# Ten GpSimd no-operations in place of a memset between two row gathers in a graph layer on one Trainium2 core

## The chip, the cores and the metric

The kernel runs on one core of one Trainium2 chip. The metric is the device time of one execution in microseconds (us). Several executions are timed and their median is given; a separate execution is recorded by the hardware profiler, with the start and end of every instruction on every engine. TensorE (PE) multiplies matrices, VectorE (DVE) and ScalarE (ACT) do elementwise work, GpSimd (POOL) issues the indirect transfers, and SyncE (SP) issues the other transfers.

## The reference

The reference is one graph layer with a residual and a layer norm over 12,500 nodes of 128 features and 412,500 edges (200,000 random pairs in both directions and one loop for each node), sorted by the destination `dst`.

```python
theta = x[dst] - x[src]
w = sigmoid(relu(theta @ W1 + b1) @ W2 + b2)
agg = segment_sum(w * theta, dst, num_segments=n_nodes)
indeg = segment_sum(ones((dst.shape[0], 1)), dst, num_segments=n_nodes)
out = layernorm(x + agg + indeg * (x @ W4 + b4))
```

The random access is `x[src]`: for each edge a row of 128 features, and its product with `W1`, are needed beside the edge's other data.

## The kernel before

**Table.** The kernel first writes a table `z` to HBM with a row of 256 numbers for each node: `x @ W1` and `x`, side by side (1,024 bytes). It is made in chunks, by transposes and products on PE and copies on ACT.

**Parts.** The edges are worked in 260 parts, numbered `s`, from 0 to 259. The first 26 (`PLAIN`) hold 1,024 edges each in plain order. The other 234 hold 1,656 edges each: those whose source lies in a hot group of nodes that is kept in SBUF (`tabs`) are reached with one-hot products on PE, and the rest with gathers. Two parts make a block of destination nodes, which is normalised and written out at the block's end.

**Gathers.** The function `gather(s)` issues the row gathers of part `s`: eight indirect transfers on POOL for each part, but two for the last one. One gather brings 128 rows, one for each partition, into slot `k` of a buffer. The parts below `NH` = 8 gather 128 numbers a row straight from `x` while the table is still being written: 64 gathers, called x gathers here. All later parts gather 256 numbers a row from `z`: 2,010 gathers, called z gathers here, of which 144 belong to parts 8 to 25 and 1,866 to the parts from 26 on. The last 1,866 stand in the profile with the index tile `src_i`, the 144 with `src`.

**The rest.** Between each gather and the next, in all parts, `gather(s)` puts one more instruction on POOL, `rest` in the code. For an x gather it is one `engine_nop`, for a z gather a memset of the tile `rest_t`, 128 partitions by 320 float32 numbers, which nothing reads. A dependency without a semaphore (`NoSync`) fixes the order of gather, rest, gather on POOL.

**What sets the order around it.** POOL runs its instructions in the order in which they stand. In the main loop, `part(s)` with `s` from 26 on, `gather(s + LEAD)` is issued with `LEAD` = 3, so rows are fetched three parts ahead. Two things hold a gather back: its buffer, one of six (`zbuf`, a ring), must have been read by the part that used it before; and the first gather of a part waits for a recent PE instruction (`paced[s + LEAD] = newest[0]`), so that POOL cannot run far ahead. The orders of PE, DVE and ACT are written out by hand; the part's first DVE instruction on the gathered rows is at L896 (`nc.vector.tensor_sub(half, ...)`), and the last PE instructions on them are the sums at L1083. Beside the parts, DVE and ACT sort the edges of the next 128 parts into the hot and the gathered ones (`place`), a few instructions at a time.

Of the kernel before, what the change touches and what calls it, by code (L numbers as in the profile page):

```python
# [9 lines left out]
F32 = mybir.dt.float32  # L10
# [10 lines left out]
P = 128  # L21
# [19 lines left out]
NH = 8  # L41
# [39 lines left out]
def gnn_resnorm(  # L81
# [37 lines left out]
    nc = tc.nc  # L119
# [21 lines left out]
    const = ctx.enter_context(tc.tile_pool(name="const", bufs=1))  # L141
# [14 lines left out]
    def set_of(s):  # L156

        s0 = 0 if s < PLAIN else PLAIN + (s - PLAIN) // S2 * S2
        return placed[s0], s - s0
# [42 lines left out]
    def early(n, dtype=F32):  # L202

        a = used_of[0]
        used_of[0] = a + -(-n // (2 if dtype == BF16 else 1))
        assert used_of[0] <= HR * HT * D
        t = tabs_flat[:, a:used_of[0]]
        return t if dtype == F32 else t.bitcast(dtype)
# [47 lines left out]
    rest = early(D)  # L256
# [82 lines left out]
    def slots(s):  # L339
        return [h * J + j for h in range(2) for j in range(pairs(s))]  # L340
# [11 lines left out]
    def rows_of(s):  # L352
        return own_of(s)[:, :, :D] if s < NH else ring(s)[:, :, :2 * D]
# [8 lines left out]
        nc.vector.memset(zbuf[i][:, :, D + AW - 1:D + AW], 1.0)  # L362

    gathers = []
    rest_t = const.tile([P, 320], F32, name="rest_t")
    table_steps = []
    paced = {}

    def gather(s):

        (src_i, _, _), i = set_of(s)
        for k in slots(s):
            if gathers:
                rest = nc.gpsimd.memset(rest_t, 0.0) if s >= NH else nc.gpsimd.engine_nop()  # L374
                tc.add_manual_dep(
                    rest.ins, gathers[-1].ins.name,
                    mybir.DependencyInfo(mybir.DependencyClass.NoSync, mybir.DependencyReason.DATA),
                    reason="between two gathers")
                gathers.append(rest)
            ins = nc.gpsimd.indirect_dma_start(  # L380
                out=rows_of(s)[:, k, :], out_offset=None, in_=z if s >= NH else x,
                in_offset=IndirectOffsetOnAxis(ap=src_i[:, k, i:i + 1], axis=0))
            waits = [(gathers[-1], mybir.DependencyClass.NoSync)] if gathers else []
            at = (s * K + k) * 4 * len(chunks) // (NH * K) - 6
            if s < NH and 0 <= at < len(table_steps):
                waits.append((table_steps[at], mybir.DependencyClass.Sync))
            if k == 0 and s in paced:
                waits.append((paced[s], mybir.DependencyClass.Sync))
            for other, kind in waits:
                tc.add_manual_dep(  # L390
                    ins.ins, other.ins.name,
                    mybir.DependencyInfo(kind, mybir.DependencyReason.DATA), reason="gathers' pace")
            gathers.append(ins)
# [283 lines left out]
    with tc.manual_schedule(engines={SP}), tc.tile_pool(name="work", bufs=2) as wp, tc.tile_pool(  # L677
        name="ps_y", bufs=2, space=bass.MemoryType.PSUM
    ) as ps_y, tc.tile_pool(
        name="ps_l", bufs=1, space=bass.MemoryType.PSUM  # L680
# [518 lines left out]
        def gather_first():  # L1199

            while gathered[0] < AHEAD and (gathered[0] + 1) * len(chunks) <= (len(done) + 1) * NH:
                gather(gathered[0])
                gathered[0] += 1
# [63 lines left out]
        def early_part(s):  # L1267
# [21 lines left out]
            if h == 1:  # L1289
                load_dst((s + 3) // SUB)  # L1290
            gather(s + AHEAD)
            one_hot_w(s)
            logits(s)
# [49 lines left out]
        def part(s):  # L1343
# [26 lines left out]
            if PLAIN + AHEAD <= s + LEAD < NS:  # L1370
                if s >= PLAIN + 4:
                    paced[s + LEAD] = newest[0]
                gather(s + LEAD)
# [233 lines left out]
```

## Time and profile before

| what | value |
|---|---|
| median of 3 runs | 3409.33 us (3401.54 to 3410.72) |
| profiled execution, device time | 3395.38 us |
| its span, first to last instruction | 3393.6 us |
| mean granted TensorE clock | 0.885 |
| start of the first gather of part 26 | 386.90 us |
| start of the last gather | 3344.44 us |

A row of the timeline gives the start and the duration in us, the engine, the line of the kernel, the operation, the tile that is written and those that are read, the shape, and in brackets how long the engine was idle before it and what ended that. A row of the groups gives the number of instructions behind the x, then the busy time in us, the mean duration in ns, and behind the second bar the idle time of the engine before them with what ended it. POOLq is the sequencer of POOL: what stands there is not counted as busy time of the engine. "issue" marks idle time for which the profile shows no wait.

### The profile page before, as it was taken

The page shows a single profiled execution, that of the slowest core. Times are in us where ns is not written, and L with a number is a line of the kernel's source. Part 1 is how long each engine was busy: PE and PEld are TensorE (multiplying, and loading weights), DVE is VectorE, ACT ScalarE, POOL GpSimd, SP SyncE. Part 2 cuts the span into 40 slices and gives each one's busy share as a digit, 9 for nine tenths or more (in the row PEclk, how much of TensorE's full clock was granted, in tenths as well). Part 3 has the DMA queues.
Part 4 walks back from the last instruction along what each step waited for, and adds up shares of the span by engine and source line. Part 5 has one row for each costly group of instructions (what it writes and reads, how often), then busy time and mean ns, then how long its engine had stood idle before and what let it go on. Part 6 is the DMA issues. An engine that isn't in the chain of part 4 may idle for free.

```text
span 3393.6 us, 62355 instructions
## 1 busy us (share of the span) xinstructions
PE 2713.4 (80%) x18615; PEld 2351.2 (69%) x18615; DVE 2641.6 (78%) x6197; ACT 2363.5 (70%) x5856; POOL 2821.6 (83%) x4093
## 2 busy tenths in 40 slices
PE   6776778787788787888788878888878888888887
PEld 5676767676677676777677766676667777677776
DVE  6797458898888689888888858888887866666666
ACT  4554567776677677777777767777767777777774
POOL 5678778888888888888888888888888888888883
PEclk9876678898899888999898889899988999998998
DMA  7564434444444444444444444444444444444441
GB/s 255 184 169 121 119 93 121 118 111 117 121 113 120 128 113 116 121 117 121 122 118 120 116 118 123 117 117 124 116 115 123 115 122 117 119 122 118 126 110 55
DMA packets 265060, 416.67 MB, mean 123 GB/s; under 512 B 66608, under 2 KB 178217, under 8 KB 264205
## 3 DMA queue, kind: packets, MB, share of 16 engines
q0 software_dynamic: 98528, 267.78, 28.5%
q1 hardware_dynamic: 164219, 138.42, 15.6%
q10 hardware_dynamic: 1970, 6.40, 0.5%
q8 instruction: 154, 2.52, 0.3%
q14 instruction: 189, 1.55, 0.2%
HBM read 384.89 MB, written 27.49 MB: 122 GB/s over the span
## 4 chain that ended last, share of the span: by engine, by line
DVE 30%; ACT 25%; PE 16%; issue 11%; POOL 8%; DMA 5%; another core or an unknown queue 4%; DVEq 0%; SPq 0%; POOLq 0%; ACTq 0%
POOL zbuf L380 6%; ACT wxh L1063 5%; PE pd L980 4%; DVE hh L1054 4%; DVE zbuf L896 4%; DVE zbuf L898 4%; ACT zbuf L919 4%; DVE lg L899 4%; ACT of L966 4%; PE pa L1083 4%; POOL rest_t L374 2%; DMA zbuf<-z,src_i 2%; ACT of L968 2%; DVE ed L549 2%
## 5 line engine op out<-in xcount | busy, mean ns | idle before, releaser
L380 POOL DMA_INDIRECT zbuf<-z,src_i x1866 | 1816.1, 973 | 421.0 <-issue 261.6
L980 PE MATMUL pd<-of,tabs 128*128 128x128 f32 (+4 forms) x4816 | 685.9, 298 | 181.6 <-ACT of L968 95.8
L374 POOL MEMSET rest_t<- 128x320 f32 x2010 | 800.4, 398 | 1.0
L980 PEld LDWEIGHTS pd<-of,tabs 128*128 128x128 f32 x4816 | 628.9, 209 | 224.7 <-ACT of L968 113.5
L1083 PE MATMUL pa<-zbuf,ow 128*112 128x260 f32 (+1 forms) x2282 | 588.1, 406 | 47.6 <-ACT zbuf L919 21.6
L1083 PEld LDWEIGHTS pa<-zbuf,ow 128*112 128x112 f32 x2282 | 407.4, 200 | 157.7 <-ACT zbuf L919 30.1
L1025 PE MATMUL pxa<-wni,xT 128*128 128x128 f32 x1872 | 303.8, 311 | 258.0 <-DVE hh L1054 241.5
L1025 PEld LDWEIGHTS pxa<-wni,xT 128*128 128x128 f32 x1872 | 266.1, 218 | 281.8 <-DVE hh L1054 261.0
L966 ACT ACTIVATE of<-hot_src,nodes 128x512 f32<-128x512 f16 (+3 forms) x602 | 394.1, 709 | 7.1 <-issue 4.3
L919 ACT ACTIVATE zbuf<-zbuf 128x128 f32<-128x128 f32 x1144 | 362.8, 389 | 0.4
L1040 PE MATMUL y<-y,oh 64*128 64x128 f32 x1872 | 341.1, 323 | 14.2 <-issue 14.0
L1029 PE MATMUL pxa<-y,oh 64*128 64x128 f32 x1872 | 336.9, 323 | 9.9 <-issue 9.6
L1054 DVE SCALAR_TENSOR_TENSOR hh<-pxa,w_r 128x128 f32<-128x128 f32 x936 | 270.7, 289 | 92.9 <-remote 48.2
L1083 PEld LDWEIGHTS pa<-wxh,owh 128*112 128x112 f32 x2340 | 295.2, 177 | 34.8 <-issue 12.6
L968 ACT ACTIVATE of<-of 128x1024 f32<-128x1024 f32 (+3 forms) x301 | 310.8, 1033 | 9.2
L1083 PE MATMUL pa<-wxh,owh 128*112 128x130 f32 x2340 | 308.9, 276 | 5.8 <-issue 4.4
L994 ACT ACTIVATE xT<-pd 128x512 f32<-128x512 f32 (+7 forms) x496 | 185.7, 416 | 183.2 <-PE pd L980 59.5
L1029 PEld LDWEIGHTS pxa<-y,oh 64*128 64x128 f32 x1872 | 275.2, 219 | 49.5 <-issue 26.9
L928 DVE TENSOR_TENSOR zbuf<-zbuf,fix 128x512 f32<-128x512 f32 x234 | 160.2, 684 | 186.4 <-ACT fix L903 118.9
L896 DVE TENSOR_TENSOR zbuf<-y,zbuf 128x1024 f32<-128x1024 f32 x234 | 285.5, 1220 | 13.5 <-issue 3.5
L898 DVE SCALAR_TENSOR_TENSOR zbuf<-zbuf,fix 128x1024 f32<-128x1024 f32 x234 | 285.7, 1221 | 8.0
L899 DVE TENSOR_REDUCE lg<-zbuf 128x8 f32<-128x1024 f32 x234 | 285.5, 1220 | 8.0
(265 smaller groups left out, 4710.0 us busy)
## 6 DMA issues: line engine op xcount, KB each, us to landing
to_all<-off_d SPq DMA_DIRECT2D x234, 144.0 KB
hot_src<-hot_s SPq DMA_DIRECT2D x257, 128.0 KB
zbuf<-z,src_i POOLq DMA_INDIRECT x1866
z<-zbuf SPq DMA_DIRECT2D x8, 1024.0 KB
xw<-in_x_dram SPq DMA_DIRECT2D x130, 56.0 KB
u<-u_d SPq DMA_DIRECT2D x130, 56.0 KB
out_dram<-o SPq DMA_DIRECT2D x130, 56.0 KB
y<-z SPq DMA_DIRECT2D x252, 28.0 KB
```

Source lines behind the costliest of these rows:

```text
L374: rest = nc.gpsimd.memset(rest_t, 0.0) if s >= NH else nc.gpsimd.engine_nop()
L380: ins = nc.gpsimd.indirect_dma_start(out=rows_of(s)[:, k, :], out_offset=None, in_=z if s >= NH else x, in_offset=IndirectOffsetOnAxis(ap= ...
L896: nc.vector.tensor_sub(half, yy.to_broadcast([P, 2, J, D]), half)
L898: nc.vector.scalar_tensor_tensor(h, h, 0.0, w2.to_broadcast([P, K, D]), op0=OP.max, op1=OP.mult)
L899: nc.vector.tensor_reduce(lg[:, :, 0], h, AX.X, OP.add)
L919: nc.scalar.activation(wx[:, k, :D], wx[:, k, :D], AF.Copy, scale=wx[:, k, D:D + 1])
L966: nc.scalar.activation(of[:, t, :], hot_src[:, i % NU, :w], AF.Abs, bias=nodes[:, t:t + 1])
L980: newest[0] = nc.tensor.matmul(to[:, q], tabs[:, g * RG + q, t, :], of[:, t, q], start=t == 0, stop=t == HT - 1)
L1025: nc.tensor.matmul(hot_y(s, q), xT[:, q * P:(q + 1) * P], wneg, start=q % G == 0, stop=False, skip_group_check=True)
L1029: newest[0] = nc.tensor.matmul(hot_y(s, q), d["oh"][:, BP + q * P:BP + (q + 1) * P], y_of(s), start=False, stop=True, skip_group_check=True)
L1054: nc.vector.scalar_tensor_tensor(h, hot_y(s, q), 0.0, w2_r, op0=OP.max, op1=OP.mult, accum_out=lg[:, q, :])
L1083: newest[0] = nc.tensor.matmul(to if len(w.shape) == 3 else to[:, 0, :], one, w, start=first and i == 0, stop=last and i == len(terms) - 1)
```

## The change

For z gathers, ten `engine_nop` instructions stand where the memset stood; for x gathers the single one stays. The tile `rest_t` is gone.

```diff
     gathers = []
-    rest_t = const.tile([P, 320], F32, name="rest_t")
...
             if gathers:
-                rest = nc.gpsimd.memset(rest_t, 0.0) if s >= NH else nc.gpsimd.engine_nop()
-                tc.add_manual_dep(
-                    rest.ins, gathers[-1].ins.name,
-                    mybir.DependencyInfo(mybir.DependencyClass.NoSync, mybir.DependencyReason.DATA),
-                    reason="between two gathers")
-                gathers.append(rest)
+                for _ in range(10 if s >= NH else 1):
+                    rest = nc.gpsimd.engine_nop()
+                    tc.add_manual_dep(
+                        rest.ins, gathers[-1].ins.name,
+                        mybir.DependencyInfo(mybir.DependencyClass.NoSync, mybir.DependencyReason.DATA),
+                        reason="between two gathers")
+                    gathers.append(rest)
             ins = nc.gpsimd.indirect_dma_start(
```

On POOL, at the step from the last x gather to the first z gathers, the order changes as follows, with the semaphores that a row waits for in brackets. `ISA` is the no-operation; `DMASW` semaphores tell of earlier gathers, `DMAHW` of SP's transfers, `Pool` of POOL's own earlier instruction.

```order
 L374 ISA
 L380 DMA zbuf_171<-in_x_dram,src_68 128x128 [waits DMASW7_49,PE_49]
-L374 MEMSET rest_t 128x320
+L374 ISA x10
 L380 DMA zbuf_172<-z,src_68 128x256 [waits DMAHW4_49,DMAHW5_49,DMAHW3_49,DMAHW6_49,DMAHW1_49,DMAHW7_49,DMASW0_49,Activation_49]
-L374 MEMSET rest_t 128x320 [waits Pool_49]
+L374 ISA x10
 L380 DMA zbuf_172<-z,src_68 128x256 [waits DMASW1_49]
```

Each memset but the first waited for the memset before it; the no-operations wait for nothing. The gathers keep their order and what they wait for, and so it goes on to the last gather. The orders of PE, DVE and ACT are the same but for the number of one tile, and SP's rows differ in the numbers of HBM tiles alone.

## The prediction

> **What bounds the kernel now.** I read the page first: busy time by engine, the slices, the chain of work that ended last.
>
> ```profile
> PE 2713.4 (80%) x18615; PEld 2351.2 (69%) x18615; DVE 2641.6 (78%) x6197; ACT 2363.5 (70%) x5856; POOL 2821.6 (83%) x4093
> POOL 5678778888888888888888888888888888888883
> DVE 30%; ACT 25%; PE 16%; issue 11%; POOL 8%; DMA 5%; another core or an unknown queue 4%; DVEq 0%; SPq 0%; POOLq 0%; ACTq 0%
> POOL zbuf L380 6%; ACT wxh L1063 5%; PE pd L980 4%; DVE hh L1054 4%; DVE zbuf L896 4%; DVE zbuf L898 4%; ACT zbuf L919 4%; DVE lg L899 4%; ACT of L966 4%; PE pa L1083 4%; POOL rest_t L374 2%; DMA zbuf<-z,src_i 2%; ACT of L968 2%; DVE ed L549 2%
> ```
>
> Four engines are between 70% and 83% busy and the chain wanders over all of them. POOL is the busiest, evenly over the main loop, yet only 8% of the chain lies on it. To see how near it is to being the bound I took its groups in a stretch of the steady main loop, from 700 to 3100 us, and POOL's timeline there.
>
> ```profile
> L380 POOL DMA_INDIRECT zbuf<-z,src_i x1518 | 1481.3, 976 | 316.1 <-issue 212.7 <-PE pd L980 25.4 <-PE last L1029 20.8
> L374 POOL MEMSET rest_t<- 128x320 f32 x1518 | 605.8, 399 | 0.7
> ...
> 1499.58 0.95 POOL L380 DMA_INDIRECT zbuf<-z,src_i  x1 [0.17 <-issue]
> 1500.53 0.38 POOL L374 MEMSET rest_t<- 128x320 f32 x1
> 1501.08 0.95 POOL L380 DMA_INDIRECT zbuf<-z,src_i  x1 [0.17 <-issue]
> 1502.03 0.38 POOL L374 MEMSET rest_t<- 128x320 f32 x1
> 1502.57 0.95 POOL L380 DMA_INDIRECT zbuf<-z,src_i  x1 [0.17 <-issue]
> ```
>
> A z gather starts every 2400 / 1518 = 1.581 us. Of that, 0.976 is the gather, 0.399 the memset, and 316.1 / 1518 = 0.208 idle time. The timeline shows that 0.165 of the idle time is there after every memset, with no wait. So only 0.043 us a gather, under 3%, is time in which POOL waits for other engines. POOL has almost no slack: whatever lengthens the step from gather to gather by more than 0.043 us makes POOL the bound of the main loop, and whatever shortens it only frees an engine that is 8% of the chain.
>
> **The change part by part.** It removes 2,010 memsets and puts 20,100 no-operations in their place, so the whole question is how long ten of these keep the next gather back. The trace has one no-operation between x gathers:
>
> ```profile
> 96.11 0.95 POOL L380 DMA_INDIRECT zbuf<-in_x_dram,src  x1 [0.30 <-issue]
> 97.36 0.94 POOL L380 DMA_INDIRECT zbuf<-in_x_dram,src  x1 [0.30 <-issue]
> 98.61 0.94 POOL L380 DMA_INDIRECT zbuf<-in_x_dram,src  x1 [0.30 <-issue]
> 99.85 0.94 POOL L380 DMA_INDIRECT zbuf<-in_x_dram,src  x1 [0.30 <-issue]
> ...
> L374 POOL MEMSET rest_t<- x2010: 378/379/976, 119.1 to 3343.9; 128x320 f32 x183
> L374 POOLq ENGINE_NOP  x63: 32/32/43, 5.3 to 117.8; - x63
> ...
> L380 POOLq EVENT_SEMAPHORE  x1356: 17/17/3291, 11.3 to 3342.7; - x194
> L380 POOL DMA_INDIRECT zbuf<-in_x_dram,src x64: 938/944/2753, 4.2 to 118.1; - x64
> ...
> L380 POOL DMA_INDIRECT zbuf<-z,src_i x1866: 951/952/1652, 386.9 to 3344.4; - x187
> ```
>
> *The step with one no-operation.* X gathers follow each other every (99.85 - 96.11) / 3 = 1.247 us. A z gather's median is 952 ns against 944, so a z gather with one no-operation would come every 1.255 us. The mean z gather is 0.024 longer than its median (0.976); I keep this, since what stretches a gather is not the memset behind it. Sum: 1.279. Of the 0.043 us of waiting, some vanishes once POOL is late (the wait for PE), some may stay; between 0 and 0.043 I take 0.02. Floor of the step: 1.30 us and nine further no-operations, 9n.
>
> *The price n of a further one.* No two stand in a row in this trace, so n is bounded. From below: 17 ns, the shortest thing that POOL's sequencer does there. The no-operation's own record is 32 ns at the median, 43 at most. From above, by the memset's own time:
>
> ```profile
> 0.25 0.10 POOL L1595 MEMSET const-float32-0.0<- 128x1 f32 x1 [0.25 <-issue]
> 0.28 0.10 POOL L1595 MEMSET const-float32-1.0<- 128x1 f32 x1
> 0.31 0.11 POOL L1595 MEMSET const-bfloat16-1.0<- 128x1 bf16 x1
> 0.34 0.12 POOL L1595 MEMSET const-uint8-127<- 128x1 uint8 x1
> ...
> masks.py:197 POOL MEMSET wni<- 128x128 f32 x1 | 0.2, 204 | 0.3 <-POOLq L1595 0.3
> ...
> L1595 POOL MEMSET const-float32-0.0<- 128x1 f32 x1 | 0.1, 98 | 0.3 <-issue 0.3
> ```
>
> One-element memsets are recorded with 0.10 us but start 0.03 us apart, so POOL overlaps small instructions and one holds it for about 0.03. An element costs (204 - 98) / 127 = 0.83 ns, so the memset of 320 holds POOL for about 0.03 + 319 x 0.00083 = 0.296 us. The z step with it is 1.495 (1499.58 to 1501.08 to 1502.57), the z step with one no-operation 1.255; so a no-operation is worth 0.296 - 0.240 = 0.056 us. The same four rows speak against the far case in which each no-operation costs the whole 0.305 us gap. Between 32 and 56 ns I take 40, nearer to the instruction's own row. Then 9n = 0.36 and the step is 1.66 us, 0.08 more than now.
>
> The Trainium skill, page Perfetto Trace Analysis, section GPSIMD Engine Instruction, says that a GpSimd instruction which reads no tensor has only a single reported point in time, and that one should go by the spacing of starts and not by the reported duration. The memsets above, 0.10 us long and 0.03 apart, agree. By that rule the 32 ns mean little and the spacing argument, 56 ns, is the better reading; that is the second rival below.
>
> *What lies beside.* The no-operations touch no SBUF. A memset is stretched now and then (399 ns mean against 379), so it meets VectorE, and VectorE may wait in turn. I put this gain at nothing; the group that shows such stretching most bounds it:
>
> ```profile
> L1181 DVE TENSOR_SCALAR o<-v,mv,sd 112x128 f32<-112x128 f32 x130 | 56.2, 442 | 6.2 <-DMA out_dram<-o 6.1
> ...
> L1181 DVE TENSOR_SCALAR o<-v,mv,sd x130: 312/340/860, 275.9 to 3387.8; 112x128 f32<-112x128 f32 x130
> ...
> q8 instruction: 154, 2.52, 0.3%
> q14 instruction: 189, 1.55, 0.2%
> ```
>
> (442 - 340) x 130 is 13 us of VectorE in all, not all of it due to memsets nor on the path. The program also grows: 4.07 MB were loaded for 62,355 instructions, 65 bytes each, so 18,090 more are 1.2 MB, from 0.5% to about 0.65% of the DMA engines' time. I cost that at nothing, covered by loading ahead; if it came late, POOL would stand still and the time would rise. The semaphore by which each memset waited for the one before falls away; it never held anything (0.7 us idle before 1,518 memsets).
>
> *What is late next.* A gather queued behind ten no-operations is late, and the gathers behind it. First the lead is used up: the rows now lie ready for some time before VectorE reads them. Ends of that lead:
>
> ```profile
> 122.62 0.95 POOL L380 DMA_INDIRECT zbuf<-z,src  x1 [3.16 <-DMA z<-zbuf]
> ...
> 2748.10 0.95 POOL L380 DMA_INDIRECT zbuf<-z,src_i  x1 [0.16 <-issue]
> ...
> 2756.32 1.23 DVE L896 TENSOR_TENSOR zbuf<-y,zbuf 128x1024 f32<-128x1024 f32 x1
> ...
> 3344.44 0.95 POOL L380 DMA_INDIRECT zbuf<-z,src_i  x1 [0.17 <-issue]
> ...
> L896 DVE TENSOR_TENSOR zbuf<-y,zbuf x234: 1200/1224/1251, 413.4 to 3369.4; 128x1024 f32<-128x1024 f32 x117
> ```
>
> Counted by parts, the L896 at 2756.32 belongs to the gather at 2748.10: 8.2 us, among the shortest leads. The last part has 25.0. At 0.08 us a gather, 17 us of lead are gone after some 210 gathers, 27 parts; from then on VectorE waits at L896 for rows, and the other engines, in their written order, behind it.
>
> *The sum.* First gather of part 26 at 386.9, as now (the 144 earlier z gathers come every (386.9 - 122.6) / 144 = 1.84 us and have room). Then 1,866 x 1.66 = 3097.6. Then from the last gather to the end, now 3393.6 - 3344.4 = 49.2, less the 17 us of lead: 32. Span 3516.5, with the 1.8 us around it (3395.4 - 3393.6) 3518: 123 us or 3.6% above the profiled execution. That execution was 14 us faster than the median of the runs; a time set by POOL's own pace should vary less, so I add almost nothing: **3520 us**.
>
> **The rivals.**
>
> *A dear no-operation.* n is 56 ns, as the spacing argument has it. The step is 1.30 + 0.50 = 1.80 us and the time 386.9 + 3358.8 + 32 + 1.8 = 3780 us. For it: one-element memsets show that records overlap, so a record is no price. Against it: an instruction without data should cost no more than the 0.03 us of the smallest memset.
>
> *A cheap no-operation, and a faster kernel.* After a single no-operation, 0.305 - 0.032 = 0.27 us of idle time follows, after a memset only 0.165: part of the gap may be the next gather's own preparation, beside which further no-operations run for nothing. It decides below the n at which the step equals now's 1.581, n = 31 ns. With 17 ns the step is 1.45, 8% shorter. Since 8% of the chain is on POOL (271 us), that saves about 22 us, and the rest stays with the other engines: 3375 us. Hiding them completely (1.30, 18% shorter) saves up to 49 us, 3345. For it: the unexplained 0.1 us of the gap. Against it: with n = 0.032 there is nothing to gain, and the no-operation is recorded behind the gather, not beside it.
>
> *No net change.* n is 28 to 33 ns, so ten no-operations equal the memset with its gap within the 0.043 us of slack: 3400 to 3420 us, at 3409. For it: the record of 32 ns and the memsets' spacing of 0.03 us both lie just there. Against it: POOL would then have no slack at all, and each late gather would stay late.
>
> That the ten would be merged into fewer is excluded by the order on POOL, which has them all.
>
> **How the numbers follow.** The forecast, n of 33 to 48 ns, reaches from 3420 to 386.9 + 1866 x 1.732 + 33.8 = 3653 us; chance 0.42. The dear no-operation, beyond that, 0.24. No net change 0.14. The faster kernel 0.20. The range reaches from 3380, into the faster case, to 3800, just beyond the dear one's price; it leaves out nearly complete hiding and an n over 57 ns. About 0.3% is what a measurement of this kernel can tell from no change, so slower has 0.42 + 0.24 = 0.66, within 0.3% 0.14, faster 0.20.
>
> **What would show it.** The start-to-start time of z gathers within a part: 1.62 to 1.64 if the forecast holds (1.255 + 0.36), 1.50 or less if the no-operations are cheap, 1.76 if dear. POOL's idle time before the gathers should then have no more waits for PE pd L980, and VectorE should wait for the gathers at L896 in most parts. The chain should lie on POOL for well over half of the span. I would be wrong if no-operations in a row have another price than the one alone, if instruction loading stops POOL, or if VectorE gains more without the memset than its rows show.

## The result, and the profile after

| | before | after |
|---|---|---|
| median of 4 runs each | 3405.43 us (3399.63 to 3410.72) | 3463.01 us (3448.91 to 3474.58) |
| profiled execution: span | 3393.6 us | 3461.8 us |
| mean granted clock | 0.885 | 0.886 |
| first gather of part 26 / last gather, start | 386.9 / 3344.4 us | 404.5 / 3412.9 us |

The changed kernel takes 1.0172 times as long, 95% interval 1.0150 to 1.0193. The forecast was 3520 us, slower. The sign came true and the time lies in the range, but the way there was another one than forecast, as the profile after shows. First its page, with busy time by engine, POOL's slices and the chain that ended last:

```profile
PE 2762.3 (80%) x18615; PEld 2368.4 (68%) x18615; DVE 2609.1 (75%) x6197; ACT 2368.0 (68%) x5856; POOL 2020.7 (58%) x2083
POOL 5546556656656656566656656665655666565652
ACT 27%; PE 25%; DVE 24%; issue 11%; another core or an unknown queue 6%; DMA 4%; POOL 2%; SPq 1%; POOLq 1%; DVEq 0%; ACTq 0%
```

POOL is busy for 58% instead of 83% of the span and holds 2% of the chain instead of 8%: it did not become the bound. PE went from 16% to 25% of the chain. Next POOL's timeline in the main loop and its gathers from 700 to 3100 us (groups: count, busy, mean ns, idle before and its reasons):

```profile
1501.34 0.95 POOL L380 DMA_INDIRECT zbuf<-z,src_i  x1 [0.87 <-remote]
1502.74 0.95 POOL L380 DMA_INDIRECT zbuf<-z,src_i  x1 [0.45 <-issue]
1504.13 0.95 POOL L380 DMA_INDIRECT zbuf<-z,src_i  x1 [0.45 <-issue]
1505.84 0.95 POOL L380 DMA_INDIRECT zbuf<-z,src_i  x1 [0.76 <-issue]
1507.23 0.95 POOL L380 DMA_INDIRECT zbuf<-z,src_i  x1 [0.45 <-issue]
1508.62 0.95 POOL L380 DMA_INDIRECT zbuf<-z,src_i  x1 [0.45 <-issue]
...
L380 POOL DMA_INDIRECT zbuf<-z,src_i x1493 | 1452.5, 973 | 948.7 <-issue 608.7 <-remote 58.4 <-ACT zbuf L919 55.4
```

An undisturbed step is 1.39 us, *shorter* than the 1.495 us with the memset. Ten no-operations leave POOL idle for 0.445 us between two gathers (median of all rows) where one left 0.305, so a further one lengthens the step by (0.445 - 0.305) / 9 = 0.016 us. Their starts lie 0.021 us apart in the trace, so nine of them take 0.19 us, and about 0.05 us of that runs beside idle time that was there anyway. Yet a gather starts on average only every 2400 / 1493 = 1.607 us (before: 1.581). POOL is early and then waits for others: the gather at 1501.34 had to wait for a semaphore that the profile puts on no engine ("remote"), and that at 1505.84 was 0.31 us late with no wait found.

Where did the time go? The waits of PE point to it (engine, line, what was waited for: us in total, times, longest). "issue" is idle time for which the view finds nothing that ended a wait within the last 1 us. Before:

```profile
PE pxa L1025 <- DVE hh L1054: 241.5, 98, 9.3
PE pd L980 <- issue: 82.7, 108, 4.7
PE pa L1083 <- issue: 15.5, 40, 2.8
```

and after:

```profile
PE pxa L1025 <- DVE hh L1054: 141.5, 72, 8.5
PE pd L980 <- issue: 125.9, 161, 10.1
PE pa L1083 <- issue: 55.3, 173, 1.0
```

PE now waits 100 us less for VectorE at L1025, and stands still for longer where the view finds no reason. The sum of all rows "PE ... <- issue" of this view is 193.3 us before and 289.7 after, 96 us more; it is called PE's **unexplained idle time** below. It is a mixture: 137.1 us of it before and 185.5 after stand ahead of matmuls that do have a semaphore to wait for, L980 above all, and 37.8 and 26.0 us of that were waiting in fact, for events that came more than 1 us ahead of the start; 56.2 and 104.3 us stand ahead of matmuls with none. Stops of over 1 us (up to 10.1) make up 113 us before and 126 after, so most of what was added is in short stops. Several of these often follow each other, as in PE's timeline after:

```profile
1653.32 1.05 PE L1025 MATMUL pxa<-wni,xT 128*128 128x128 f32 x7
1654.76 0.36 PE L1025 MATMUL pxa<-wni,xT 128*128 128x128 f32 x1 [0.38 <-issue]
1655.49 0.27 PE L1029 MATMUL pxa<-y,oh 64*128 64x128 f32 x1 [0.37 <-issue]
...
1656.34 0.27 PE L1040 MATMUL y<-y,oh 64*128 64x128 f32 x1 [0.21 <-issue]
1657.08 0.39 PE L1029 MATMUL pxa<-y,oh 64*128 64x128 f32 x2 [0.47 <-issue]
1657.87 0.35 PE L1040 MATMUL y<-y,oh 64*128 64x128 f32 x1 [0.40 <-issue]
```

Matmuls of which seven otherwise take 1.05 us start 0.7 us apart. PE's idle time in all grew by only 19 us (680.2 to 699.5), its busy time by 49: a matmul that stands alone is recorded with 0.27 to 0.36 us in these rows, so part of the loss may be counted as busy. Of the 68 us of longer span, 18 us were lost ahead of the main loop (386.9 to 404.5) and 51 in it (2957.5 us from the first of its gathers to the last before, 3008.4 after). From the last gather to the end it takes 3461.8 - 3412.9 = 48.9 us, as before (49.2), so VectorE's lead over the gathers did not shrink either.

### The profile page after: what moved, and what is told of

It is laid out like the page before. It is cut to its first block, busy times and chain, and to the rows that moved or that the text cites. A ratio compares the mean times of both kernels' runs of the same rounds, so it can differ in the third digit from the quotient of the medians.

```text
span 3461.8 us, 80445 instructions
## 1 busy us (share of the span) xinstructions
PE 2762.3 (80%) x18615; PEld 2368.4 (68%) x18615; DVE 2609.1 (75%) x6197; ACT 2368.0 (68%) x5856; POOL 2020.7 (58%) x2083
## 3 DMA queue, kind: packets, MB, share of 16 engines
q0 software_dynamic: 98528, 267.78, 27.7%
## 4 chain that ended last, share of the span: by engine, by line
ACT 27%; PE 25%; DVE 24%; issue 11%; another core or an unknown queue 6%; DMA 4%; POOL 2%; SPq 1%; POOLq 1%; DVEq 0%; ACTq 0%
PE pd L980 7%; PE pa L1083 6%; ACT wxh L1063 5%; ACT of L966 5%; ACT zbuf L919 4%; DVE zbuf L896 3%; DVE zbuf L898 3%; DVE lg L899 3%; DVE hh L1054 3%; ACT of L968 3%; PE pxa L1029 3%; ACT xT L994 2%; POOL zbuf L380 2%; PE pxa L1025 2%
## 5 line engine op out<-in xcount | busy, mean ns | idle before, releaser
L980 PE MATMUL pd<-of,tabs 128*128 128x128 f32 (+4 forms) x4816 | 708.1, 303 | 210.9 <-issue 125.9
L980 PEld LDWEIGHTS pd<-of,tabs 128*128 128x128 f32 x4816 | 650.5, 214 | 256.5 <-issue 163.8
L1083 PE MATMUL pa<-zbuf,ow 128*112 128x260 f32 (+1 forms) x2282 | 612.8, 412 | 63.5 <-ACT zbuf L919 29.3
L1083 PEld LDWEIGHTS pa<-zbuf,ow 128*112 128x112 f32 x2282 | 413.3, 204 | 194.9 <-issue 58.8
L1025 PE MATMUL pxa<-wni,xT 128*128 128x128 f32 x1872 | 291.4, 304 | 172.7 <-DVE hh L1054 141.5
L1025 PEld LDWEIGHTS pxa<-wni,xT 128*128 128x128 f32 x1872 | 257.5, 212 | 195.8 <-DVE hh L1054 157.7
L1083 PE MATMUL pa<-wxh,owh 128*112 128x130 f32 x2340 | 328.5, 279 | 34.2 <-issue 32.9
L1083 PEld LDWEIGHTS pa<-wxh,owh 128*112 128x112 f32 x2340 | 303.3, 179 | 74.5 <-issue 53.3
L1040 PE MATMUL y<-y,oh 64*128 64x128 f32 x1872 | 322.3, 312 | 16.6 <-issue 15.8
L1029 PE MATMUL pxa<-y,oh 64*128 64x128 f32 x1872 | 316.2, 311 | 12.2 <-issue 12.0
L896 DVE TENSOR_TENSOR zbuf<-y,zbuf 128x1024 f32<-128x1024 f32 x234 | 285.5, 1220 | 13.8 <-issue 5.9
L1029 PEld LDWEIGHTS pxa<-y,oh 64*128 64x128 f32 x1872 | 260.9, 210 | 48.3 <-issue 24.8
L838 ACT ACTIVATE oh<-to_all,away,mine 128x1152 f32<-128x1152 bf16 x117 | 157.2, 1344 | 199.8 <-remote 170.3
```

The source lines that it names most:

```text
L896: nc.vector.tensor_sub(half, yy.to_broadcast([P, 2, J, D]), half)
L980: newest[0] = nc.tensor.matmul(to[:, q], tabs[:, g * RG + q, t, :], of[:, t, q], start=t == 0, stop=t == HT - 1)
L1025: nc.tensor.matmul(hot_y(s, q), xT[:, q * P:(q + 1) * P], wneg, start=q % G == 0, stop=False, skip_group_check=True)
L1029: newest[0] = nc.tensor.matmul(hot_y(s, q), d["oh"][:, BP + q * P:BP + (q + 1) * P], y_of(s), start=False, stop=True, skip_group_check=True)
L1083: newest[0] = nc.tensor.matmul(to if len(w.shape) == 3 else to[:, 0, :], one, w, start=first and i == 0, stop=last and i == len(terms) - 1)
```

## The experiments

The question was why a POOL that is quicker between two gathers makes PE stop. The first four kernels separate four theories. PLACES: without `rest_t` 71 of the tiles lie 1,280 bytes lower, and that does it. REST: the shorter time between gathers does it, by whatever it is filled. INSTRUCTIONS: nine further instructions a gather, or their loading, do it. MEMSET: the memset itself has to be there. "Stalls" in the expectations are worked out from all rows of a trace: the sum of the distances between neighbouring matmuls that start at least 0.5 us apart, where the second has no semaphore to wait for (98 us before, 192 with the change). It orders the runs as the unexplained idle time does, except among those between 254 and 290 us of it and for the lowest two. The first four ran on a chip where the kernel before needs 3361.16 us, the rest where it needs 3403 to 3406; ratios are always to the runs beside them.

**The change with the tile kept.**

```diff
+    rest_t = const.tile([P, 320], F32, name="rest_t")
...
+                for _ in range(10 if s >= NH else 1):
+                    rest = nc.gpsimd.engine_nop()
```

> Ten no-operations as in the change, but the tile that the memset wrote stays reserved, so that every tile has its old place in SBUF; nothing else differs from the change. Theory PLACES (the 71 tiles that moved down by 1280 bytes cost the time): as before, a ratio of 1.00. Theories REST (a rest of another length between two gathers costs it), INSTRUCTIONS (the 18,090 further POOL instructions cost it) and MEMSET (a memset does something that no-operations do not): as the change, a ratio of 1.015 to 1.02 to before.

Measured: 3422.06 us, ratio 1.0177 (1.0147 to 1.0207), as the change itself, with unexplained idle time of 254 us. PLACES falls.

**A shorter memset, no no-operations.**

```diff
-                rest = nc.gpsimd.memset(rest_t, 0.0) if s >= NH else nc.gpsimd.engine_nop()
+                rest = nc.gpsimd.memset(rest_t[:, :200], 0.0) if s >= NH else nc.gpsimd.engine_nop()
```

> The kernel before with the memset cut from 320 to 200 columns: 120 x 0.83 ns less, so an undisturbed step between gathers of 1.395 us, that of the change (1.394), with the instruction count of before. REST: as the change, 1.015 to 1.02. INSTRUCTIONS: as before or a little faster, 0.99 to 1.00, since POOL's step is shorter. MEMSET: as before or in between, up to 1.01. PLACES: 1.00.

Measured: 3427.58 us, ratio 1.0214 (1.0173 to 1.0256). POOL's timeline has a step of 1.40 us:

```profile
1500.89 0.96 POOL L380 DMA_INDIRECT zbuf<-z,src_i  x1 [0.17 <-issue]
1501.84 0.28 POOL L374 MEMSET rest_t<- 128x200 f32 x1
1502.29 0.96 POOL L380 DMA_INDIRECT zbuf<-z,src_i  x1 [0.17 <-issue]
```

and PE stops as in the changed kernel:

```profile
PE pd L980 <- issue: 75.0, 94, 2.5
PE pa L1083 <- issue: 73.6, 155, 2.4
```

This kernel has not one instruction more than the kernel before, and its memset is there. A rest that is 0.1 us shorter suffices for the whole loss: INSTRUCTIONS and MEMSET (in the form that any memset will do) are not needed, REST stands.

**One no-operation, the shortest rest.**

```diff
-                rest = nc.gpsimd.memset(rest_t, 0.0) if s >= NH else nc.gpsimd.engine_nop()
+                rest = nc.gpsimd.engine_nop()
```

> One no-operation between all gathers, tiles in their old places: an undisturbed step of about 1.25 us, the instruction count of before. REST: slower than the change, 1.03 or more, since the rest is shorter still. INSTRUCTIONS: not slower than before, 0.98 to 1.00. MEMSET: as the change, 1.015 to 1.02. PLACES: 0.99 to 1.00.

Measured: 3940.7 us, ratio 1.1746 (1.1705 to 1.1787), granted clock 0.804. POOL's timeline, in one burst of eight gathers (the line numbers of some kernels are one or two higher for the same code):

```profile
2020.17 0.95 POOL L381 DMA_INDIRECT zbuf<-z,src_i  x1 [8.24 <-PE pd L981]
2021.42 0.94 POOL L381 DMA_INDIRECT zbuf<-z,src_i  x1 [0.30 <-issue]
...
2028.94 0.95 POOL L381 DMA_INDIRECT zbuf<-z,src_i  x1 [0.30 <-issue]
```

and PE's timeline at the end of this burst:

```profile
2026.91 0.62 PE L1022 MATMUL pxb<-wni,xT 128*128 128x128 f32 x2
2028.64 0.27 PE L1022 MATMUL pxb<-wni,xT 128*128 128x128 f32 x1 [1.10 <-issue]
2029.37 0.27 PE L1022 MATMUL pxb<-wni,xT 128*128 128x128 f32 x1 [0.46 <-issue]
2030.09 0.46 PE L1022 MATMUL last<-wni,xT 128*128 128x128 f32 x1 [0.46 <-issue]
2030.80 0.37 PE L1026 MATMUL last<-wni,xT 128*128 128x128 f32 x1 [0.25 <-issue]
2031.51 0.57 PE L1026 MATMUL last<-wni,xT 128*128 128x128 f32 x1 [0.33 <-issue]
...
2032.73 3.81 PE L1084 MATMUL pa<-zbuf,ow 128*112 128x260 f32 x8
```

After some 7 us of gathers every 1.25 us, PE gives out one matmul in 0.72 us; from 2032.73 on, 3.8 us after the burst's last gather started, matmuls follow each other without idle time again. POOL, for its part, had waited 8.24 us for PE ahead of this burst and waits 3.19 us ahead of the next: nothing is won by being early. PE's unexplained idle time is 616.9 us, 424 more than in the profile before, against the 580 us that the kernel is slower (3940.70 - 3361.16). The lower clock is not what makes PE stop: it was granted at half for 39% of the span, but only 17% of the unexplained idle time falls there (in the changed kernel 23% and 10%). What the lower clock adds to the time was not separated.

**Fifteen no-operations.**

```diff
-                for _ in range(10 if s >= NH else 1):
+                for _ in range(15 if s >= NH else 1):
```

> Fifteen no-operations, tiles in their old places: 5 x 0.021 us more, so an undisturbed step of 1.498 us, that of the memset of 320 columns (1.495), with 28,000 further POOL instructions. REST: as before, 1.00. INSTRUCTIONS: slower than the change by half as much again, about 1.025 to 1.03. MEMSET: as the change or slower, 1.015 to 1.03. PLACES: 1.00.

Measured: 3671.38 us, ratio 1.0917 (1.0899 to 1.0935); REST had expected 1.00. PE hardly stops any more (52.0 us of unexplained idle time), but now POOL is late, and VectorE waits for it. First VectorE's wait in the kernel before, then POOL's timeline, VectorE's wait and the chain in this one:

```profile
DVE zbuf L896 <- DMA zbuf<-z,src_i: 2.0, 8, 0.4
```

```profile
1505.50 0.94 POOL L381 DMA_INDIRECT zbuf<-z,src_i  x1 [0.83 <-issue]
1507.31 0.94 POOL L381 DMA_INDIRECT zbuf<-z,src_i  x1 [0.86 <-DVE ew L548]
1508.80 0.95 POOL L381 DMA_INDIRECT zbuf<-z,src_i  x1 [0.55 <-issue]
...
DVE zbuf L897 <- DMA zbuf<-z,src_i: 589.2, 188, 11.4
...
DVE 42%; ACT 20%; issue 14%; DMA 12%; PE 7%; POOL 3%; POOLq 1%; DVEq 1%; SPq 1%; ACTq 0%; another core or an unknown queue 0%
```

The undisturbed step is 1.49 us as planned (idle 0.55, so five further no-operations cost 0.10, 0.020 each), but in the slots 4 to 7 it is about 1.78 (idle 0.83). The gathers of those slots wait for two semaphores, and the second wait is an instruction of its own. So this run did not test REST at equal pace; it shows the forecast's mechanism, gathers that come too late, in a kernel with half as many no-operations again. Even here the chain lies on POOL for 3% only, so a chain mostly on POOL, which the forecast named as its mark, was no good sign of it: the lateness shows in VectorE's wait, and in the chain as transfers (DMA 12%) and "issue" (14%).

**Half the bytes.** One no-operation everywhere, and rows of `x`:

```diff
-                out=rows_of(s)[:, k, :], out_offset=None, in_=z if s >= NH else x,
+                out=rows_of(s)[:, k, :D], out_offset=None, in_=x,
```

> One no-operation between all gathers (undisturbed step 1.25 us, as in the run with ratio 1.1746), and every z gather takes the 512-byte row of x in place of the 1024-byte row of z: the same number of rows and descriptors, half the bytes. The part left out is x@W1 in the gathered rows: they hold x and old data there. TRAFFIC (the bytes of a burst of gathers, while they land, hold TensorE's instructions up): the stalls of TensorE without a recorded wait fall to below 150 us from 588, and the ratio to 0.98 to 1.03. ISSUE (the cadence in which GpSimd issues gathers does it, whatever they carry): stalls above 450 us and a ratio of 1.14 to 1.18. In between (1.05 to 1.12) the packets count, not the bytes alone.

Measured: 4031.69 us, ratio 1.185 (1.183 to 1.187), 650.0 us of unexplained idle time. Half the bytes bring nothing; how often POOL issues a gather of 128 rows counts. The packets that carry data fell by half as well, from 32 to 16 a z gather (the page of each run has the queue's packets: 98,528 and 66,368, with 16 short ones of 4 bytes in each gather), so the packets do not explain the stops either. Whether the descriptors stayed the same in number, as was expected, the trace does not show.

**Longer memsets.**

```diff
-    rest_t = const.tile([P, 320], F32, name="rest_t")
+    rest_t = const.tile([P, 352], F32, name="rest_t")
```

The longer tile also moves the tiles behind it; the first run, with the same time in either place, speaks against that as a cause.

> The memset of before, 352 columns in place of 320: undisturbed step about 1.522 us, 0.027 more. REST (a rest that is too short makes TensorE stall; the time has its least where stalls and POOL's own pace meet): stalls of TensorE fall from 98 us to 30 to 80; POOL's step still fits below 1.581, so the ratio is 0.990 to 1.002. PACE (POOL has no room left, each 0.027 us more counts): 1866 x 0.02 us of lateness is 37 us, ratio 1.008 to 1.015.

Measured: 3387.67 us, ratio 0.9956 (0.9939 to 0.9973), 101.2 us of unexplained idle time. REST's expectation holds, also in the size (45 us of stalls). And with 384 columns:

> One memset of 384 columns: undisturbed step about 1.549 us, 0.053 more than before. REST (stalls fall further with the length of the rest): below 45 us of stalls, the figure with 352 columns (ratio 0.9956). What then decides is POOL's own pace: with 352 columns the mean step was 1.580, 0.054 above the undisturbed one; if that waiting can shrink to 0.03 the mean step stays at 1.58 and the ratio is 0.993 to 0.999; if it stays at 0.054 the step is 1.603, 1866 x 0.022 = 41 us more, less 20 us of lead, ratio 1.000 to 1.008 (PACE).

Measured: 3392.15 us, ratio 0.9958 (0.9944 to 0.9972). POOL's timeline, PE's waits and the chain with 384 columns:

```profile
1500.95 0.95 POOL L380 DMA_INDIRECT zbuf<-z,src_i  x1 [0.16 <-issue]
1501.90 0.43 POOL L374 MEMSET rest_t<- 128x384 f32 x1
1502.50 1.10 POOL L380 DMA_INDIRECT zbuf<-z,src_i  x1 [0.16 <-issue]
...
PE pxa L1025 <- DVE hh L1054: 401.9, 145, 9.9
PE pd L980 <- issue: 37.5, 39, 6.9
...
DVE 34%; POOL 19%; ACT 18%; issue 11%; PE 9%; DMA 7%; another core or an unknown queue 1%; DVEq 1%; SPq 0%; POOLq 0%; ACTq 0%
```

With a step of 1.55 us PE's unexplained idle time is down to 86.7 us and PE waits for VectorE instead; POOL's share of the chain has risen from 8% to 19%. These two kernels beat both the kernel before and the changed one, by about 0.4% of the former. From one to the other, what PE wins POOL loses: the ratio stays the same. Longer single memsets were not tried.

**The length made up with no-operations.** A memset of 200 columns and five no-operations, step 1.505 us, with the no-operations behind the memset and then ahead of it:

```diff
+                for n in range(6 if s >= NH else 1):
+                    rest = nc.gpsimd.memset(rest_t[:, :200], 0.0) if s >= NH and n == 0 else nc.gpsimd.engine_nop()
```

> A memset of 200 columns (alone: step 1.400, ratio 1.0214) followed by five no-operations of 0.021 us each: undisturbed step about 1.50 us, as before. REST (only the length of the rest counts, however it is made): ratio 0.995 to 1.006, stalls of TensorE 80 to 120 us. MEMSET (a memset of less than 320 columns is what costs, or the no-operations as such): ratio 1.015 to 1.03. SUPPLY (more instructions on POOL's queue than it can be fed, as with fifteen no-operations): seven or eight instructions a gather at about 0.1 us each are 0.8 us, below the step, so it does not bind; if it did, the step would be above 1.55 and the ratio above 1.03.

Measured: 3460.78 us, ratio 1.016 (1.0126 to 1.0194), 258.3 us of unexplained idle time. Two of PE's waits:

```profile
PE pd L981 <- issue: 79.3, 105, 6.7
PE pa L1084 <- issue: 51.4, 155, 2.4
```

REST in the form "only the length counts" falls: the step is 0.01 us longer than before, and the loss stays. With `n == 5` in place of `n == 0`:

> The five no-operations ahead of the memset of 200 columns instead of behind it; the same instructions, step about 1.50 us. PLACE IN THE STEP (what stands directly ahead of the next gather counts, a memset being better than a no-operation): ratio 0.995 to 1.008, stalls 80 to 120 us. NO-OPS and MEMSET: as with the no-operations behind, ratio 1.012 to 1.02, stalls 180 to 240 us.

Measured: 3474.48 us, ratio 1.019 (1.0151 to 1.0229), 291.8 us. PLACE IN THE STEP falls: the loss is there with the no-operations on either side, and the two intervals overlap.

**Long and short rests in turn.**

```diff
-    rest_t = const.tile([P, 320], F32, name="rest_t")
+    rest_t = const.tile([P, 640], F32, name="rest_t")
...
-                rest = nc.gpsimd.memset(rest_t, 0.0) if s >= NH else nc.gpsimd.engine_nop()
+                rest = nc.gpsimd.memset(rest_t, 0.0) if s >= NH and k % 2 else nc.gpsimd.engine_nop()
```

> A memset of 640 columns before every second gather, one no-operation before the others: steps of about 1.76 and 1.25 us in turn, 1.505 on average, as before. AVERAGE (a backlog that builds up over several gathers makes TensorE stall, so the mean cadence counts): ratio 0.995 to 1.01, stalls of TensorE 80 to 130 us. PAIR (each gather that starts within about 1.4 us of the one before costs by itself): half the gathers have a step of 1.25, so about half of the loss with one no-operation everywhere, ratio 1.06 to 1.10, stalls 250 to 350 us.

Measured: 3404.52 us, ratio 0.9999 (0.9987 to 1.0012), 172.4 us. Steps of 1.26 and 1.76 us in turn do as well as 1.50 throughout: it is the mean over at least two gathers that counts, as AVERAGE had it, and PAIR falls.

**The length made up with a second memset.**

```diff
+                for n in range(2 if s >= NH else 1):
+                    rest = nc.gpsimd.memset(rest_t[:, :(84 if n else 200)], 0.0) if s >= NH else nc.gpsimd.engine_nop()
```

> The memset of 200 columns followed by a second one of 84 columns, no no-operations: undisturbed step about 1.50 us, as before and as with 200 columns and five no-operations (ratio 1.016, 208 us of stalls of TensorE). NO-OPS (more instructions without data on GpSimd's queue make TensorE stall, beside the cadence): without them the stalls are back at 80 to 120 us and the ratio at 0.995 to 1.006. MEMSET (one memset of 320 columns or more is what keeps TensorE running, because of its own length): stalls above 160 us, ratio 1.012 to 1.025. COUNT (each further instruction of any kind counts): one more of five, ratio about 1.003, stalls about 120 us.

Measured: 4039.69 us, ratio 1.1863 (1.1843 to 1.1882). No theory had this. The second memset writes the tile of the first and waits for it, and the steps grew to 1.61 us in the slots 1 to 3 and 2.01 in the slots 4 to 7. POOL's timeline and VectorE's first wait:

```profile
1502.80 0.50 POOL L375 MEMSET rest_t<- 128x200 f32 x2
1503.46 0.95 POOL L381 DMA_INDIRECT zbuf<-z,src_i  x1 [0.15 <-issue]
1504.41 0.50 POOL L375 MEMSET rest_t<- 128x200 f32 x2
1505.47 0.95 POOL L381 DMA_INDIRECT zbuf<-z,src_i  x1 [0.56 <-issue]
...
DVE zbuf L897 <- DMA zbuf<-z,src_i: 927.5, 220, 12.4
```

POOL is late as with fifteen no-operations, and the question stayed unanswered. So once more with two tiles, where the second memset has nothing to wait for:

```diff
-    rest_t = const.tile([P, 320], F32, name="rest_t")
+    rest_t = const.tile([P, 200], F32, name="rest_t")
+    rest_u = const.tile([P, 120], F32, name="rest_u")
...
+                    rest = nc.gpsimd.memset(rest_u[:, :84] if n else rest_t, 0.0) if s >= NH else nc.gpsimd.engine_nop()
```

> As the run with two memsets (200 and 84 columns, ratio 1.1863), but into two tiles, so that the second need not wait for the first; no no-operations, undisturbed step about 1.50 us if the wait between the two was what made that step 1.61 and 2.01. NO-OPS (time filled with no-operations does not keep TensorE running, time filled with memsets does): stalls of TensorE 60 to 130 us, ratio 0.995 to 1.006. ONE LONG MEMSET (what counts is the length of a single memset): stalls above 160 us, ratio 1.012 to 1.025. THIRD INSTRUCTION (any further instruction beside the separate wait of the slots 4 to 7 holds their gather back, with or without a wait between the memsets): step 1.50 in slots 1 to 3 but above 1.75 in slots 4 to 7, hardly any stalls, ratio above 1.10.

Measured: 3415.85 us, ratio 1.0034 (1.0020 to 1.0048), 202.6 us of unexplained idle time, steps of 1.505 us in all slots. The wait between the two memsets was what had made POOL slow. The time falls to what NO-OPS expected; the stalls are 134 us, just above its 130 and below the 160 of ONE LONG MEMSET. At this step one instruction more costs 0.34%, five cost 1.6 to 1.9%, so the theory COUNT (named with the run before), which had 1.003 and 120 us for one more, fits as well.

**All together**, by the undisturbed step:

| rest between z gathers | step, us | PE's unexplained idle time, us | ratio |
|---|---|---|---|
| 1 no-operation | 1.25 | 616.9 | 1.1746 |
| 10 no-operations, the change | 1.39 | 289.7 | 1.0172 |
| memset 200 | 1.40 | 274.1 | 1.0214 |
| memset 320, before | 1.495 | 193.3 | 1 |
| memset 640 or 1 no-operation in turn | 1.505 mean | 172.4 | 0.9999 |
| memsets 200 and 84, two tiles | 1.505 | 202.6 | 1.0034 |
| memset 200, 5 no-operations | 1.505 | 258.3 | 1.0160 |
| 5 no-operations, memset 200 | 1.505 | 291.8 | 1.0190 |
| memset 352 | 1.526 | 101.2 | 0.9956 |
| memset 384 | 1.549 | 86.7 | 0.9958 |
| 15 no-operations | 1.49 and 1.78 | 52.0 | 1.0917 |
| memsets 200 and 84, one tile | 1.61 and 2.01 | 36.7 | 1.1863 |

Counted only ahead of matmuls that have no semaphore to wait for, PE's idle time is 56.2 us before, 104.3 with the change, 105.0 with the memset of 200 columns and 409.0 with one no-operation, 24.4 and 2.9 with 352 and 384 columns, and 0 in the last two rows: the picture is the same without the mixture.

The time has its least between two limits: with shorter steps PE stops, with longer ones POOL is late. The kernel before stood close to that least, on PE's side.

## Why the forecast came out right, and where it was wrong

**The price of a no-operation failed.** The prediction took 40 ns, between 32 and 56. It is 16 ns from the tenth back to the first and 20 ns for five more. Neither 32 nor 56 ns was a price: the record of 32 ns overlaps the next one, and the 56 ns rested on the time that a memset was thought to hold POOL. The lower bound of 17 ns came nearest, but it is the row of another instruction (a semaphore wait), so that it lies so near may be chance. The Trainium skill's rule (page Perfetto Trace Analysis, section GPSIMD Engine Instruction), to go by the spacing of starts and not by a reported duration, agrees with this trace: the no-operations start 21 ns apart and are recorded with 32 ns. What misled was the spacing of other instructions, the small memsets.

**POOL as the bound failed with it.** The mark for this was a step of 1.62 to 1.64 us; 1.39 was found, which the prediction had named as the mark of cheap no-operations. Accordingly there is no chain on POOL (2%, well over half forecast), the waits of POOL for PE did not vanish, VectorE waits only 13.8 us at L896, and the lead of the gathers is whole (48.9 us at the end against the 32 forecast). In the sum 386.9 + 3097.6 + 32 the terms measured are 404.5, 3008.4 and 48.9.

**The sentence that cost most** stood in the first part: whatever shortens the step "only frees an engine that is 8% of the chain". Its other half, that 0.043 us more would make POOL the bound, does not hold either: the memset of 384 columns lengthened the undisturbed step by 0.054 us, and the kernel became 0.4% faster. The rival of cheap no-operations was right about the undisturbed step (1.45 us or less) and rested on the same sentence; it gave 3345 to 3375 us, 90 to 120 too little. A step 0.1 us shorter is no gain here but a loss of 2%, as the memset of 200 columns shows with no no-operation at all. What had been in the trace before: PE had 82.7 us of idle time at L980 for which the view finds no cause, 108 times. The prediction quoted L980 only as something that POOL waits for and did not ask what PE itself was waiting for.

**That the kernel is slower**, and that the time lies in the range, was therefore luck: the reason was wrong, and the size (3.4% forecast, 1.7% measured) is that of another mechanism. No net change and the dear no-operation fall with the price.

**What was costed at nothing.** The further instructions were loaded as reckoned (queue q14 went from 1.55 to 2.70 MB, 1.15 MB more for 1.2 reckoned):

```profile
q14 instruction: 330, 2.70, 0.3%
```

POOL now and then stands still between two no-operations without a wait, as before the gather at 1505.84: 359 times, 201 us in all. That this is late loading is not shown: 30 of the 359 overlap a packet of q14, and with fifteen no-operations, where q14 moves 3.40 MB, there are 96. VectorE gained: its busy time fell from 2641.6 to 2609.1 us, and nothing of it shows in the time. The first gather of part 26 was put at 386.9 us "as now" and came at 404.5; in the stretch from 120 to 410 us POOL's waits for PE pa L1083 doubled:

```profile
POOL zbuf L380 <- PE pa L1083: 22.7, 25, 4.5
```

before, and after:

```profile
POOL zbuf L380 <- PE pa L1083: 46.9, 26, 9.6
```

What makes those sums late in that stretch was not followed up.

**What stays open.** Shown is that more frequent gathers on POOL make PE stop (four widths of memset and the single no-operation, in order), that the mean frequency counts and the bytes do not, and that at an equal step no-operations bring the stops back. Not shown is how PE and POOL meet. The gathers' descriptors are one place where it could be: the Trainium skill, page DMA: Bandwidth & Descriptors, section Terms, says that those of GpSimd's transfers are written to rings in SBUF; no run here shows that path, or counts the descriptors. Nor is it known what a uniform step as long as the forecast's 1.66 us would have cost: the runs that came nearest, with fifteen no-operations and with two memsets in one tile, had uneven steps. The two influences, step and number of instructions, also do not add up: ten no-operations at 1.39 us cost no more than a memset alone at 1.40. The pauses between no-operations (201 us in the change), which spread the gathers, may be the reason; that is only argued.

## What to carry to other kernels

An instruction that does nothing but pass time may be there to hold an engine back for the sake of another: before making it cheaper, ask who is disturbed when the engine runs ahead, and look for idle time without an explanation on the other engines. A filler is set by trying its length in both directions, since the best one lies where two opposite losses meet (here 352 to 384 columns, 0.4% below the tuned 320), and here one long instruction did better than several short ones. A time inside the forecast range says little; the marks named beforehand (step, chain, waits) showed within one view that the reason was wrong.

## What the hardware did that was not expected

PE, undisturbed by any recorded wait, gave out one matmul in 0.72 us for 3 us on end while gathers followed each other every 1.25 us. At a step of 1.5 us the stops keep time with the gathers: worked out from all rows, 65 of 98 stops (distances of 0.55 to 0.9 us between two matmuls' starts) in the main loop before, and 166 of 256 with the 200 columns and five no-operations behind them, end 0.6 to 0.8 or 1.3 to 1.5 us after a gather's start, that is in 27% of the step. At 1.4 us the same stretches hold only 46 of 217 in the changed kernel and 14 of 136 with the memset of 200 columns alone; in the changed kernel 83 of the 217 end 0.7 to 1.0 us after a start instead.

A no-operation of GpSimd costs 0.016 to 0.020 us in a row, with starts 0.021 us apart. A gather that has a second wait as an instruction of its own comes no later behind ten of them (idle 0.45 us in both cases), but 0.28 us later behind fifteen (idle 0.83 against 0.55 us), and 0.41 us later behind two memsets of which the second waits for the first (0.56 against 0.15), while behind one memset, or two that do not wait for each other, it comes no later at all.
